# Decoder layer, last entry's self attention: where in the stage of scores the maxima's row transposes of two head groups stand

## Chip, core and metric

One core of a Trainium2 chip runs the whole kernel in one launch. The metric is the device time in microseconds (us), median of three executions. The engines are TensorE (PE; PEld is its weight load), VectorE (DVE), ScalarE (ACT), GpSimd (POOL) and SyncE (SP).

## What is computed

A decoder layer on `x` of 4 entries x 512 rows x 512 columns, float32: a causal self attention of 16 heads of 32 columns, a causal cross attention in which the context is both key and value (no projections), and a feed-forward part with a shared branch and one expert, each behind a layer norm and added to `x`. The part that the change touches is the self attention:

```python
q = (x @ q_w.T + q_b).reshape(Bd, Td, NH, HD).transpose(0, 2, 1, 3)
k = (x @ k_w.T + k_b).reshape(Bd, Td, NH, HD).transpose(0, 2, 1, 3)
v = (x @ v_w.T + v_b).reshape(Bd, Td, NH, HD).transpose(0, 2, 1, 3)
scores = jnp.einsum('bhqd,bhkd->bhqk', q, k) * SCALE
scores = jnp.where(causal, scores, -jnp.inf)
probs = jax.nn.softmax(scores, axis=-1)
ctx = jnp.einsum('bhqk,bhkd->bhqd', probs, v)
```

## The kernel before

The four entries (b = 0 to 3) run one after the other. The 16 heads of an entry form four groups g = 0 to 3 of four heads; 512 rows are four blocks of 128. The order of every engine's instructions is the order in which the program issues them: there is no scheduler, and an instruction that waits holds all that stands behind it on its engine.

An attention computes its scores twice, in two stages.

`with_maxima` is the stage of the maxima. For ten units of blocks it computes scores with query rows on the partitions (`sm`, L286), copies them to SBUF on ACT (L297), masks the diagonal on POOL (L305) and takes each row's maximum on DVE, negated (`nm`, L317). Between the units it places matmuls of other work as a filling. When the maxima of a group are complete, `split` (L339 to L343) on DVE writes each of them as three bfloat16 parts into `parts[g % 2]`. `rows(g)` then turns these parts into rows: four PE transposes of 128x128 into one PSUM tile (`mt`, L349) and one copy to SBUF (`mrow`, L355). Groups 0 and 1 are turned inside this stage, and group 2 too where the filling is long enough; `late` names the rest.

`attend` is the stage of the scores. It has ten units, here called u0 to u9, of blocks (g, j):

| unit | blocks | unit | blocks |
|---|---|---|---|
| u0 | (0,0) | u5 | (2,0) |
| u1 | (0,3) (0,1) | u6 | (2,3) (2,1) |
| u2 | (0,2) (1,2) | u7 | (2,2) (3,2) |
| u3 | (1,0) | u8 | (3,0) |
| u4 | (1,3) (1,1) | u9 | (3,3) (3,1) |

For each unit `scores` issues the transposed scores (`sc`, L383) in two PSUM tiles, a and b, adds `mrow` of the unit's groups by a matmul with ones (L394), takes the exponential on ACT (L414, into `pt`, or into `sum` for block 0 of groups 0 to 2), and masks the diagonal on POOL (L422). The values of unit n, here v0 to v9 (`pv`, L453), stand behind the scores of unit n + 2. The softmax denominators of groups 0 to 2 are summed first on DVE (`add_up`, L483: each block of a group is added into `sum`), and then over the partitions by one matmul with ones, `summed` (L489). `summed(0)` stands at the end of v2, `summed(1)` at the end of v5, `summed(2)` (`ls`) in v8.

`attend` issues the row transposes that `late` names right behind the scores of a unit, and their copy on ACT behind that unit's exponentials:

```python
for n, pieces in enumerate(units):
    waiting.append(a.scores(pieces))
    if n in late:
        for copy in a.rows(late[n]):
            copy(nc.scalar.copy)
    if len(waiting) > 2:
        values()
```

In entries 0 to 2 `late` is `{3: 3}`. In entry 3 the filling of the maxima stage is 16 matmuls for ten units, which is less than `2 * len(units)`, so group 2 is left for `attend` too.

All PSUM tiles come from one pool of four buffers of two banks each. A new tile takes the buffer that has been free longest, and its first writer on PE waits until the last reader of the old tile is done.

Of the kernel before, what the change touches and what calls it, by code (L numbers as in the profile page):

```python
# [26 lines left out]
def decoder_layer(  # L27
# [26 lines left out]
    NC = D // P  # L54
# [776 lines left out]
    def run(steps):  # L831
        for step in steps:
            for _ in step() or ():
                pass

    def matmuls(steps):

        for step in steps:
            yield from step() or ()
            yield  # L840

    def with_maxima(steps, a, first=0, norms=()):


        norms = list(norms)
        run(steps[:first])
        fill = matmuls(steps[first:])
        total = sum(1 if step.__name__ in ("share", "gate") else NC for step in steps[first:])

        units = []  # L850
        for g in range(0, NC, 2):
            units += [[(g, 1), (g + 1, 1)]]
            units += [u for k in (g, g + 1) for u in ([(k, 2), (k, 0)], [(k, NT - 1)])]

        lead = 2 if first else 0
        for _ in range(lead):
            next(fill)
        done, due, jobs, late = lead, float(lead), [], {3: NC - 1}
        for n, pieces in enumerate(units):
            new = a.maxima(pieces)  # L860
            if norms and n % 2 == 0:
                new.append(norms.pop(0))
            due += (total - lead) / len(units)

            count = round(due) - done
            for k in range(count):
                next(fill, None)
                done += 1
                if k == min(1, count - 1) and n in (5, 7):
                    jobs = a.rows((n - 5) // 2) + jobs  # L870
                if n == len(units) - 1 and k == count - (2 if count > 4 else 1):
                    if total >= 2 * len(units):
                        a.rows(2)[0](nc.scalar.copy)
                    else:
                        late[1] = 2
                run(jobs[:1])
                jobs = jobs[1:]
            run(jobs)
            jobs = new
        for _ in fill:  # L880
            pass
        run(jobs)
        return late
# [35 lines left out]
    with tc.manual_schedule(engines=BY_HAND):  # L919
# [11 lines left out]
        for b in range(B):  # L931
# [3 lines left out]
            if more:  # L935
                after, norms, turns = norm_in(b + 1)
            late = with_maxima(between_self, sa, skip, norms)
            if b == B - 1:
                e.x = load_x(b)
# [9 lines left out]
            ca = Attention(e.cq_t, e.ck_t, e.cv, True, f"c{b}")  # L949
            ca.e = e  # L950
            late = with_maxima(steps[3:], ca)
            if b + 2 < B:
                after.x = load_x(b + 1)
# [77 lines left out]
```

## Time and profile before

| | us |
|---|---|
| median of 3 runs | 814.12 (813.93 to 814.19) |
| the profiled execution, its own time | 814.14 |
| its span from first to last instruction | 812.4 |
| PE busy | 800.8 (99%) |
| DVE busy | 536.7 (66%) |
| ACT busy | 397.7 (49%) |
| POOL busy | 294.6 (36%) |
| from 620 to 636 us: PE, DVE, ACT, POOL busy | 13.37, 13.77, 13.22, 8.82 |
| from 636 to 653 us: PE, DVE, ACT, POOL busy | 17.00, 15.25, 10.65, 12.34 |

The stretch from 620.7 to 652.7 us is the stage of the scores of the last entry's self attention. The granted TensorE clock is 1.00 in all stretches. PE's busy share hides short waits, since the ends of matmuls are modelled and the groups overlap; a wait is found in the list of waits, in the gap that stands at the end of a row of the timeline, or by laying one entry's rows beside another's.

### The profile page before, as it was taken

What the parts mean: (1) busy time and instruction counts of PE and PEld (TensorE: products, weight loads), DVE (VectorE), ACT (ScalarE), POOL (GpSimd) and SP (SyncE); (2) the same over time, 40 slices, a digit from 0 to 9 for tenths busy, and PEclk for the clock granted to TensorE, in tenths of its full rate; (3) what the DMA queues carried; (4) which work ended last, traced back from release to release, by engine and by line L of the source; (5) the groups of instructions that cost most, each with busy time, mean ns of one, the idle gap of its engine ahead of it and who ended that gap; (6) DMA issues with size and microseconds to landing.
All of it is one profiled execution on the core that took longest, in us unless ns stands there. A gap on an engine that the chain in (4) does not pass through costs nothing.

```text
span 812.4 us, 14289 instructions
## 1 busy us (share of the span) xinstructions
PE 800.8 (99%) x5808; PEld 382.0 (47%) x5808; DVE 536.7 (66%) x927; ACT 397.7 (49%) x450; POOL 294.6 (36%) x489
## 2 busy tenths in 40 slices
PE   8999999999999999999999999999999999999998
PEld 7444554444444454444544445444444444444544
DVE  2478835868678834586867783687779844987512
ACT  2457426862546514556145752686168714574110
POOL 4334612342234732234233482244235643353100
PEclk9999999999999999999999999999999999999999
DMA  9611000001000000030100000000102000000101
GB/s 335 235 27 28 1 1 1 1 2 53 1 27 27 2 1 1 0 106 2 52 14 14 1 2 0 1 1 2 53 16 68 23 1 0 1 2 2 52 0 52
DMA packets 13681, 24.52 MB, mean 30 GB/s; under 512 B 1968, under 2 KB 2224, under 8 KB 13616
## 3 DMA queue, kind: packets, MB, share of 16 engines
q1 hardware_dynamic: 13184, 22.96, 8.3%
q8 instruction: 45, 0.74, 0.4%
q10 hardware_dynamic: 432, 0.66, 0.2%
q14 instruction: 20, 0.16, 0.1%
HBM read 19.42 MB, written 4.19 MB: 29 GB/s over the span
## 4 chain that ended last, share of the span: by engine, by line
PE 89%; DVE 8%; ACT 2%; DMA 0%; issue 0%; ACTq 0%
PE pm_qk L235 13%; PE pv_c L453 9%; PE pm_u L235 7%; PE pm_o L663 7%; PE pm_v L223 6%; PE pm_e L223 6%; PE sc_c L383 5%; PE pv_s L453 5%; PE pm_d L223 5%; PE sm_s L286 5%; PE sm_c L286 5%; PE sc_s L383 4%; DVE nm_s L317 3%; DVE nm_c L317 2%; PE sc_c L394 1%; PE sc_s L394 1%
## 5 line engine op out<-in xcount | busy, mean ns | idle before, releaser
L317 DVE TENSOR_REDUCE nm_c<-s_c 128x2 f32<-128x1024 f32 (+3 forms) x128 | 96.0, 811 | 37.4 <-POOL s_c L305 37.4
L317 DVE TENSOR_REDUCE nm_s<-s_s 128x2 f32<-128x1024 f32 (+3 forms) x128 | 96.9, 810 | 35.2 <-POOL s_s L305 35.2
L297 ACT COPY s_s<-sm_s 128x1024 f32<-128x1024 f32 x80 | 77.1, 1015 | 64.4 <-PE sm_s L286 34.9
L297 ACT COPY s_c<-sm_c 128x1024 f32<-128x1024 f32 x80 | 77.1, 1016 | 44.5 <-PE sm_c L286 24.5
L414 ACT ACTIVATE pt_c<-sc_c 128x1024 f32<-128x1024 f32 x80 | 76.7, 1030 | 30.1 <-PE sc_c L394 29.4
L305 POOL TENSOR_SCALAR_AFFINE_SELECT s_c<-s_c 128x512 f32<-128x512 f32 (+1 forms) x80 | 44.1, 552 | 115.0 <-ACT s_c L297 115.0
L422 POOL TENSOR_SCALAR_AFFINE_SELECT pt_c<-pt_c 128x512 f32<-128x512 f32 (+1 forms) x80 | 56.0, 706 | 67.0 <-ACT pt_c L414 66.5
L305 POOL TENSOR_SCALAR_AFFINE_SELECT s_s<-s_s 128x512 f32<-128x512 f32 (+1 forms) x80 | 43.8, 551 | 90.7 <-ACT s_s L297 90.7
L483 DVE TENSOR_TENSOR sum_s<-sum_s,pt_s 128x256 f32<-128x256 f32 (+2 forms) x72 | 58.7, 879 | 14.6 <-PE pv_s L453 14.6
L223 PE MATMUL pm_d<-wdown_sb,hT 128*128 128x512 f32 x128 | 60.9, 608 | 0.0
L414 ACT ACTIVATE pt_s<-sc_s 128x1024 f32<-128x1024 f32 x56 | 54.0, 1029 | 13.5 <-PE sc_s L394 7.9
L235 PE MATMUL pm_u<-fT,wup_sb 128*128 128x512 f32 x128 | 59.1, 605 | 0.0
L223 PE MATMUL pm_v<-wv_sb,xnT 128*128 128x512 f32 x128 | 58.8, 600 | 0.0
L663 PE MATMUL pm_o<-wo_sb,oT_s 128*128 128x512 f32 x128 | 57.8, 596 | 0.0
L235 PE MATMUL pm_qk<-xnT,wk_sb 128*128 128x512 f32 x120 | 57.3, 607 | 0.0
L223 PE MATMUL pm_e<-wexp_sb,fT 128*128 128x512 f32 x120 | 56.8, 606 | 0.0
L235 PE MATMUL pm_qk<-xnT,wq_sb 128*128 128x512 f32 x120 | 56.7, 604 | 0.0
L422 POOL TENSOR_SCALAR_AFFINE_SELECT pt_s<-pt_s 128x512 f32<-128x512 f32 (+1 forms) x56 | 47.5, 856 | 19.5 <-ACT pt_s L414 18.9
L383 PE MATMUL sc_s<-qT,kT 32*128 32x384 f32 (+3 forms) x512 | 53.0, 462 | 0.9 <-ACT sum_s L414 0.6
L383 PE MATMUL sc_c<-cqT,ckT 32*128 32x384 f32 (+3 forms) x512 | 51.4, 461 | 0.9 <-ACT pt_c L414 0.9
L286 PE MATMUL sm_s<-kT,qT 32*128 32x512 f32 (+3 forms) x512 | 47.5, 461 | 0.1
L286 PE MATMUL sm_c<-ckT,cqT 32*128 32x512 f32 (+3 forms) x512 | 46.1, 460 | 0.0
(154 smaller groups left out, 1199.8 us busy)
## 6 DMA issues: line engine op xcount, KB each, us to landing
cv<-in_ctx_dram SPq DMA_DIRECT2D x16, 256.0 KB, 4.2
out_dram<-x SPq DMA_DIRECT2D x15, 256.0 KB, 2.0
x<-in_x_dram SPq DMA_DIRECT2D x14, 256.0 KB, 3.6
xin<-in_x_dram SPq DMA_DIRECT2D x12, 256.0 KB, 2.7
wq_sb<-in_wq_dram SPq DMA_DIRECT2D x2, 512.0 KB, 6.3
wk_sb<-in_wk_dram SPq DMA_DIRECT2D x2, 512.0 KB, 7.9
wv_sb<-in_wv_dram SPq DMA_DIRECT2D x1, 1024.0 KB, 8.3
wo_sb<-in_wo_dram SPq DMA_DIRECT2D x1, 1024.0 KB, 10.0
```

What stands on the lines that cost most here:

```text
L223: nc.tensor.matmul(pm, lhsT=lhs_t[:, c, t * P : (t + 1) * P], rhs=w[:, c, :], start=(c == 0), stop=(c == NC - 1),)
L235: nc.tensor.matmul(pm, lhsT=w[:, c, f * P : (f + 1) * P], rhs=rhs_t[:, c, :], start=(c == 0), stop=(c == NC - 1),)
L286: nc.tensor.matmul(scs[r // 2][:, r % 2, c : c + (i + 1) * P], lhsT=self.q_t[h, g, i * P : (i + 1) * P], rhs=self.k_t[h, g, : (i + 1) * P] ...
L297: nc.scalar.copy(s, scs[n])
L305: nc.gpsimd.affine_select(out=diagonal, in_=diagonal, compare_op=ALU.is_ge, fill=NEG, base=0, pattern=[[0, 2], [0, len(pieces)], [-1, P]], ...
L317: nc.vector.tensor_reduce(self.nm[g][:, i, 2 * n : 2 * n + 2], made[n][:, :, c : c + (i + 1) * P], axis=AX.X, op=ALU.max, negate=True,)
L383: nc.tensor.matmul(scs[r // 2][:, r % 2, c : c + S - j * P], lhsT=self.k_t[h, g, j * P : (j + 1) * P], rhs=self.q_t[h, g, j * P :], start= ...
L414: nc.scalar.activation(pt, scs[n], AF.Exp)
L422: nc.gpsimd.affine_select(out=diagonal, in_=diagonal, compare_op=ALU.is_ge, fill=0.0, base=0, pattern=[[0, 2], [0, len(pieces)], [1, P]], ...
L453: nc.tensor.matmul(pv[r * HD : (r + 1) * HD, u, j * P :], lhsT=ones if u else self.v[:, j, h * HD : (h + 1) * HD], rhs=pts[r // 2][:, r % ...
L483: nc.vector.tensor_tensor(to, to, pts[n][:, :, c : c + S - j * P], ALU.add)
L663: nc.tensor.matmul(pms[t // 2][:, t % 2, :], lhsT=a.out[:, c, t * P : (t + 1) * P], rhs=wo_sb[:, c, :], start=(c == 0), stop=(c == NC - 1),)
```

## The change

In entry 3, and there alone, `late` goes from `{3: 3, 1: 2}` to `{3: 2, 5: 3}`. The four transposes of group 2 move on PE from behind the scores of u1 to behind those of u3, and the four of group 3 from behind u3 to behind u5; their two copies on ACT move with them. Group 2 is first used by u5 and group 3 by u7.

```diff
                 if n == len(units) - 1 and k == count - (2 if count > 4 else 1):
                     if total >= 2 * len(units):
                         a.rows(2)[0](nc.scalar.copy)
                     else:
-                        late[1] = 2
+                        late = {3: 2, 5: NC - 1}
```

No instruction is added or removed. The order on DVE, POOL and SP stays as it was; on PE two groups of four transposes move, on ACT two copies. The PSUM buffers of the tiles behind them are dealt out anew.

## Prediction

> **What bounds the kernel now.** I read the page first, then PE's waits, then the timelines of PE and DVE around the moved transposes, and last the same stage of entry 0, which has only one group of transposes in it.
>
> ```profile
> PE 800.8 (99%) x5808; PEld 382.0 (47%) x5808; DVE 536.7 (66%) x927; ACT 397.7 (49%) x450; POOL 294.6 (36%) x489
> PE 89%; DVE 8%; ACT 2%; DMA 0%; issue 0%; ACTq 0%
> ```
>
> PE is the bound nearly everywhere, so only time in which PE stands still, or work taken from PE, counts. The waits of PE:
>
> ```profile
> PE mt_s L349 <- DVE parts L343: 2.6, 2, 1.5
> ...
> PE sc_s L383 <- ACT sum_s L414: 0.6, 3, 0.2
> ```
>
> Both waits of the first line (2.6 us, two times) are the transposes that the change moves. PE's timeline there:
>
> ```profile
> 622.91 0.59 PE L394 MATMUL sc_s<-mrow_s,onesb 32*128 32x128 bf16 x8
> 624.60 0.40 PE L349 MATMUL mt_s<-identb,parts 128*128 128x128 bf16 x4 [1.10 <-DVE parts L343]
> ...
> 630.32 0.40 PE L349 MATMUL mt_s<-identb,parts 128*128 128x128 bf16 x4 [1.53 <-DVE parts L343]
> ...
> 631.65 1.15 PE L383 MATMUL sc_s<-qT,kT 32*128 32x128 f32 x16
> ...
> 632.95 1.07 PE L453 MATMUL pv_s<-pt_s,v 128*32 128x256 f32 x16
> 633.83 1.32 PE L489 MATMUL pv_s<-sum_s,ones 128*32 128x512 f32 x8
> 635.08 1.14 PE L383 MATMUL sc_s<-qT,kT 32*128 32x512 f32 x8
> ```
>
> PE stands 1.10 us before group 2 and 1.53 us before group 3. The line that decides, though, is L489, `summed(0)`: it takes 1.32 us here. What it reads comes from DVE:
>
> ```profile
> 624.42 4.71 DVE L317 TENSOR_REDUCE nm_s<-s_s 128x2 f32<-128x768 f32 x6
> 629.16 0.20 DVE L339 CAST parts<-nm_s 128x16 bf16<-128x16 f32 x1
> ...
> 630.14 3.91 DVE L483 TENSOR_TENSOR sum_s<-sum_s,pt_s 128x256 f32<-128x256 f32 x6
> 637.54 4.58 DVE L483 TENSOR_TENSOR sum_s<-sum_s,pt_s 128x512 f32<-128x512 f32 x6 [3.49 <-PE pv_s L453]
> ```
>
> DVE is behind: from 617.6 us on it works without a pause through the last maxima, then `split(3)`, then the six additions into `sum` of group 0, and ends at 630.14 + 3.91 = 634.05. L489 starts at 633.83, and its second half must wait for 634.05: that is its 1.32 us. So today both queues reach L489 together. PE's 2.63 us of waiting have cost it nothing that DVE would not have cost a little later. Entry 0, same stage:
>
> ```profile
> 73.86 0.40 PE L349 MATMUL mt_s<-identb,parts 128*128 128x128 bf16 x4
> ...
> 75.19 1.72 PE L383 MATMUL sc_s<-qT,kT 32*128 32x128 f32 x16
> ...
> 77.05 1.07 PE L453 MATMUL pv_s<-pt_s,v 128*32 128x256 f32 x16
> 77.94 1.04 PE L489 MATMUL pv_s<-sum_s,ones 128*32 128x512 f32 x8
> ```
>
> There DVE is in time, L489 takes 1.04 us, and from the first score (66.46) to L489 PE needs 11.48 us. But u4, behind the transposes, takes 1.86 us (75.19 to 77.05) where it takes 1.30 above (631.65 to 632.95): a transposes' tile occupies one of four PSUM buffers, so tile b of the next unit gets the buffer of tile b just before and waits for its exponential.
>
> **The change, part by part.** It removes and adds no instruction; DVE, POOL and SP keep their order and no DMA moves. All is set against the profiled execution (814.14 us, span 812.4; the median, 814.12, is the same within 0.02).
>
> 1. Both waits before the transposes go: -2.63 us of standing, for the moment. `split(2)` ends at 624.5 and `split(3)` at 630.3; the new places come at about 628 and 637.
>
> 2. PE up to L489. The order of PE from u0 to v2 is now that of entry 0, and the PSUM buffers repeat the same way. Entry 3's u0 starts at 620.72, its first exponential at 622.10; in entry 0 that is 67.84, so entry 0 shifted by 554.26 is the template: u2 at 623.2, transposes of group 2 at 628.1, u4 at 629.5, L489 at 77.94 + 554.26 = 632.20. PE arrives 1.63 us sooner than now; the rest of the 2.63 goes to the template's own waits for exponentials, 0.56 us of it in u4. The price of four transposes is 0.33 us on PE (630.32 to the next start), and one such group now lies before L489 instead of two.
>
> 3. DVE up to L489. The maxima do not move: a maximum of 128x1024 takes 1.21 us with a POOL mask beside it or without. `split` and the additions do care about POOL. Now u3's mask falls at 629.1 and 630.0 (entry 0: 74.87, 75.78), on `split(3)`: it took 1.10 us now, and the same four steps took 1.82 us in entry 0 beside two masks. Placed step by step against these masks I get 0.27 us more. The additions: six of them took 3.91 us here with one mask inside, 4.57 us in entry 0 with three, which is 0.2 to 0.3 us a mask. After the change u3's mask leaves them and u4's two come in (entry 0: 78.11, 79.02, so 632.4 and 633.3): one more, 0.22 us. The sum of group 0 is ready at 634.05 + 0.27 + 0.22 = 634.54.
>
> Here a rule speaks against the change. The Trainium skill, "SBUF — State Buffer", section "SBUF: two separate sides", says that VectorE with two SBUF inputs and GpSimd take a shared port pair by lock, for the whole instruction, and that the loser waits in full. The trace agrees for tiny operations: L341 took 1.20 us at 621.71, its usual 0.18 plus the rest of POOL's 1.27 us addition (L802). For the additions it does not: the rule would add up to a whole mask, 0.64 us, for each of two, 634.05 + 0.27 + 1.28 - 0.22 = 635.4; the rows say 634.5. I take the rows and keep the other for the range.
>
> 4. So PE waits at L489 for about 2 us instead, and u5 starts when the second half of L489 is through, as long after the sum as today: 635.08 + 0.49 = 635.57. The clock is no cost: it stayed at 1.00 after a stand of 2.00 us before the transposes at 8.34.
>
> 5. Transposes of group 3 behind u5: +0.33 us, now on the path, since they stand behind the new wait instead of before it.
>
> 6. Their PSUM tile. Behind the change u6 gets the two buffers of u5 (now it gets a free one and u5a's). From the transposes' start to v2 entry 0 took 77.05 - 73.86 = 3.19 us; today from u5's end (636.37) to v4 (638.83) it is 2.46. So transposes and stall cost 0.73 together, plus 0.18 because u5's exponentials start 0.10 us after that point (636.47) where u3's started 0.08 before: 0.91, of which 0.33 is counted. +0.58 us. The bounds are 0, if a buffer came free sooner, and the length of one exponential, 1.02.
>
> 7. L489 of group 1 (`summed(1)`, 642.09) took 1.06 us, of which some 0.09 was again DVE, ending at 637.54 + 4.58 = 642.12. PE now comes 1.4 us later, DVE 0.8: -0.09.
>
> 8. ACT's copies (0.59 us each): that of group 2 leaves the place before u2's exponentials, that of group 3 lies behind u5's and ends before u6's scores do. Nothing; 0.6 if it delayed u6's exponential. From u8 on PE has no gap in the timeline up to 713.57, so what is lost stays lost.
>
> Sum: 0.49 + 0.33 + 0.58 - 0.09 = +1.31 us, so 815.4.
>
> **Rivals.**
>
> A (forecast, 0.65): the wait moves to L489 and the late transposes cost what steps 5 and 6 say. Alone its range is 814.6 to 815.7 (DVE 0.2 to 0.7 later, stall 0.2 to 0.7).
>
> B (slower by more than 0.2%, 0.31): POOL's masks of u4 block DVE's additions at the rule's price. The sum of group 0 comes at 635.4, u5 at 636.4, and the total is 1.3 + 0.33 + 0.58 - 0.09 = +2.1 us, 816.2. It decides from a sum later than 634.9. For it: L341's 1.20 us, and an addition of 128x256 that took 1.5 us beside POOL's L504. Against it: the masks beside entry 0's additions.
>
> C (faster, 0.04): DVE catches up, L489 does not wait, and nothing takes the place of the 2.63 us: 811.5. With steps 2, 5 and 6 it would be -1.91 + 0.91 = -1.0, 813.1. Against it: DVE's row has no gap from 624.4 to 634.05 and its order is unchanged. That the change does nothing is excluded: PE's order differs.
>
> **Numbers.** A measurement of this kernel tells about 0.2%, 1.6 us, from no change; +1.31 lies within, close to the edge. Faster 0.04 (C), within 0.65 (A), slower 0.31 (B and A's upper end). The range 814.4 to 816.4 takes in A and B's price and leaves out C and a worse B.
>
> **What the profile would show.** Right: the waits of L349 on DVE in entry 3 are gone, a wait of about 2 us of L489 on `sum_s` L483 stands at 632 to 634.5, u5 starts near 635.6, u6's scores take about 1.9 us, the output projection starts near 654.0 instead of 652.68. Wrong: L489 of group 0 before 634; six additions of over 4.6 us (B); u6 in 1.4 us (step 6).

## Result and profile after

The changed kernel takes 815.71 us (median of 17 runs, 815.55 to 816.0) against 814.11 (17 runs, 813.93 to 814.31): +1.60 us, ratio 1.0020 with a 95% interval of 1.0012 to 1.0027. It is slower beyond its interval, and just inside the 0.2% that the prediction named as its edge. The forecast was 815.4 within 814.4 to 816.4.

The profiled execution took 816.0 us, the longest of the 17, and spans 814.3. Its first score of the stage stands at 620.98 where it stood at 620.72: 0.26 us were already lost at the very start (the first transposes came at 8.61 instead of 8.34), before anything that the change touches. Take 0.26 us off every place below to compare it with a place before.

The first line of the page, then two of PE's waits (waited for: total, times, longest):

```profile
PE 803.6 (99%) x5808; PEld 383.1 (47%) x5808; DVE 537.0 (66%) x927; ACT 397.7 (49%) x450; POOL 294.9 (36%) x489
```

```profile
PE pv_s L489 <- DVE sum_s L483: 1.4, 1, 1.4
PE sc_s L383 <- ACT sum_s L414: 1.1, 5, 0.3
```

The line of L349 on `parts` is gone. In its place stands one of L489 on the sum, and the waits of scores for exponentials grew from 0.6 us in three places to 1.1 in five. PE's timeline:

```profile
628.41 0.40 PE L349 MATMUL mt_s<-identb,parts 128*128 128x128 bf16 x4
...
634.12 2.09 PE L489 MATMUL pv_s<-sum_s,ones 128*32 128x512 f32 x8 [1.44 <-DVE sum_s L483]
636.14 1.14 PE L383 MATMUL sc_s<-qT,kT 32*128 32x512 f32 x8
...
637.43 0.40 PE L349 MATMUL mt_s<-identb,parts 128*128 128x128 bf16 x4
...
638.75 0.49 PE L383 MATMUL sc_s<-qT,kT 32*128 32x128 f32 x4
639.51 1.14 PE L383 MATMUL sc_s<-qT,kT 32*128 32x128 f32 x12 [0.27 <-ACT sum_s L414]
...
640.79 1.07 PE L453 MATMUL pv_s<-pt_s,v 128*32 128x128 f32 x16
```

PE arrives at L489 early, stands for 1.44 us, does the first half, and stands again before the second (2.09 us instead of 1.32). u5 starts at 636.14, the transposes of group 3 take their 0.33 us behind it, and u6 breaks after four matmuls until an exponential frees a PSUM buffer. DVE in the same stretch:

```profile
629.42 0.20 DVE L339 CAST parts<-nm_s 128x16 bf16<-128x16 f32 x1
...
630.21 0.23 DVE L343 TENSOR_TENSOR parts<-rest_s,parts 128x16 bf16<-128x16 f32 x1
630.31 4.79 DVE L483 TENSOR_TENSOR sum_s<-sum_s,pt_s 128x256 f32<-128x256 f32 x6
```

POOL beside the additions, before and after:

```profile
630.68 0.49 POOL L422 TENSOR_SCALAR_AFFINE_SELECT sum_s<-sum_s 128x256 f32<-128x256 f32 x1 [0.49 <-ACT sum_s L414]
```

```profile
630.34 0.68 POOL L422 TENSOR_SCALAR_AFFINE_SELECT sum_s<-sum_s 128x256 f32<-128x256 f32 x1 [0.43 <-ACT sum_s L414]
632.66 1.90 POOL L422 TENSOR_SCALAR_AFFINE_SELECT pt_s<-pt_s 128x512 f32<-128x512 f32 x2 [1.65 <-ACT pt_s L414]
```

The six additions took 4.79 us instead of 3.91. The second mask of u3 lies beside them as it did before. New are the two masks of u4, alone 0.64 us each: they lie over the end of the additions, and it is 1.90 us from the start of the first to the end of the second. The chain of work that ended last (start, us, what) says the same:

```profile
632.95 1.13 DVE sum_s L483
634.07 0.04 issue
634.12 2.09 PE pv_s L489 x8
...
637.54 1.93 ACT sum_s L414 x2
```

After the maxima and `split(3)` it now runs over DVE's additions into L489, and then through ACT's exponentials of u5 into u6. Neither was on the chain before, which went from `split(3)` to PE at 630.32 and stayed on PE through this stage.

### The profile page after: what moved, and what is told of

It reads as the page before. It is cut to its first block, busy times and chain, and to the rows that moved or that the text cites. A ratio compares the mean times of both kernels' runs of the same rounds, so it can differ in the third digit from the quotient of the medians.

```text
span 814.3 us, 14289 instructions
## 1 busy us (share of the span) xinstructions
PE 803.6 (99%) x5808; PEld 383.1 (47%) x5808; DVE 537.0 (66%) x927; ACT 397.7 (49%) x450; POOL 294.9 (36%) x489
## 4 chain that ended last, share of the span: by engine, by line
PE 89%; DVE 8%; ACT 2%; issue 0%; DMA 0%; ACTq 0%
PE pm_qk L235 13%; PE pv_c L453 9%; PE pm_u L235 7%; PE pm_o L663 7%; PE pm_v L223 6%; PE pm_e L223 6%; PE sc_c L383 5%; PE pm_d L223 5%; PE pv_s L453 5%; PE sm_s L286 5%; PE sm_c L286 5%; PE sc_s L383 4%; DVE nm_s L317 3%; DVE nm_c L317 2%; ACT sum_s L414 1%; PE sc_c L394 1%
## 5 line engine op out<-in xcount | busy, mean ns | idle before, releaser
L383 PE MATMUL sc_s<-qT,kT 32*128 32x128 f32 (+3 forms) x512 | 54.7, 463 | 1.5 <-ACT sum_s L414 1.1
```

What stands on the lines that cost most here:

```text
L383: nc.tensor.matmul(scs[r // 2][:, r % 2, c : c + S - j * P], lhsT=self.k_t[h, g, j * P : (j + 1) * P], rhs=self.q_t[h, g, j * P :], start= ...
```

## Experiments

All times are medians; the kernel before was run beside each and gave 814.13 or 814.14 us. "Theory A" is the prediction's: the sum of group 0 on DVE sets the start of u5, and what stands on PE before L489 is free. The first score of the stage starts at 620.56 to 620.98 us in these profiles, with nothing changed ahead of it, so a place is given from there where a few tenths matter.

### Group 3's transposes one unit sooner

```diff
-                        late = {3: 2, 5: NC - 1}
+                        late = {3: 2, 4: NC - 1}
```

> Late is {3: 2, 4: 3}: group 3's transposes stand behind u4, before the wait of L489, instead of behind u5. Theory A (DVE's sum of group 0 sets the start of u5; the transposes cost only where they stand behind that wait): their 0.33 us and the PSUM stall of u6 of 0.55 us disappear in the wait, so 815.7 - 0.9 = 814.8; L489 still waits for L483, by 0.33 us less, and u5 starts where it starts after the change. Rival (DVE is no bound, PE pays for every transpose and buffer wherever it stands): 815.7.

814.89 us, ratio 1.0010 (1.0002 to 1.0018): 0.82 less than the change. PE's timeline:

```profile
631.36 0.40 PE L349 MATMUL mt_s<-identb,parts 128*128 128x128 bf16 x4
631.69 1.35 PE L453 MATMUL pv_s<-pt_s,v 128*32 128x256 f32 x16
633.86 2.09 PE L489 MATMUL pv_s<-sum_s,ones 128*32 128x512 f32 x8 [0.83 <-DVE sum_s L483]
...
638.17 1.31 PE L383 MATMUL sc_s<-qT,kT 32*128 32x128 f32 x16
```

The transposes and a stall of some 0.3 us behind them (v2 takes 1.35 us instead of 1.07) go into the wait of L489, which shrinks from 1.44 to 0.83; u6 runs in one piece. Steps 5 and 6 of the prediction, the transposes and their PSUM tile, are thereby shown together: the late place costs 0.82 us, and the same work before the wait costs nothing. The 0.76 us over the kernel before that remain are left to DVE, whose additions take 4.79 us here too.

### Group 2 behind u2, group 3 left behind u3

```diff
-                        late = {3: 2, 5: NC - 1}
+                        late = {2: 2, 3: NC - 1}
```

> Late is {2: 2, 3: 3}: group 2's transposes go from behind u1 to behind u2, group 3's stay behind u3 as before the change. Theory A: the wait of 1.10 us goes, but PE then stands longer before group 3, until split(3) ends near 630.3, and L489 comes when it came: 814.1 within 0.3. Rival (each wait is PE time and is won when it goes): 814.1 - 1.1 = 813.0.

814.26 us, ratio 1.0001 (0.9993 to 1.0009). PE's waits, then its timeline:

```profile
PE mt_s L349 <- DVE parts L343: 0.7, 1, 0.7
```

```profile
633.50 1.54 PE L489 MATMUL pv_s<-sum_s,ones 128*32 128x512 f32 x8
634.97 1.14 PE L383 MATMUL sc_s<-qT,kT 32*128 32x512 f32 x8
```

1.9 us of the 2.6 us of waiting for `parts` are gone, and the time has not moved: u5 starts 14.41 us after the stage's first score, where it started 14.36 after it. These waits were worth nothing while DVE's sum stood behind them.

### Group 3 moved alone

```diff
-                        late = {3: 2, 5: NC - 1}
+                        late = {1: 2, 5: NC - 1}
```

> Late is {1: 2, 5: 3}: group 2's transposes where they stood before the change, group 3's where the change puts them. Theory A (DVE's sum of group 0 sets u5, and the loss comes from group 3's late place and from u4's masks, which come early enough to fall on the additions): PE still stands about 1.1 us before group 2, L489 waits for L483, u6's scores stall by 0.55 us, and the time is that of the whole change, 815.6. Rival (each moved group gives half of the loss): 814.9.

815.94 us, ratio 1.0028 (1.0018 to 1.0039). Three of its eight runs took 817.4, the other five 815.69 to 816.01; the profiled one took 815.70. PE's waits:

```profile
PE pv_s L489 <- DVE sum_s L483: 1.8, 1, 1.8
...
PE mt_s L349 <- DVE parts L343: 1.1, 1, 1.1
```

With group 2 back in its old place, and its old wait of 1.1 us back, the loss is whole. It is not half and half: moving group 3 alone gives all of it. That puts group 3's transposes behind the end of the sum, and it takes from PE the wait before u4, so that u4's masks come sooner and fall on the additions (4.79 us here too).

### No additions into the sum of group 0

```diff
-                if g in self.added:
+                if g in self.added and (g, self.name) != (0, "s3"):
                     for n in range(2):
```

> The changed kernel without the additions into the sum of group 0 in the last entry (left out: six DVE additions, so that entry's group 0 is divided by too small a sum). Theory A: L489 has nothing to wait for, PE runs as in entry 0, u5 starts 1.9 us before where it started before the change, and the late transposes and the stall of u6 add 0.9: 814.1 - 1.9 + 0.9 - 0.1 = 813.0. Rival (the cost sits on PE and in PSUM buffers alone, DVE is hidden): 815.7.

813.18 us, ratio 0.9988 (0.9981 to 0.9994).

```profile
632.23 1.04 PE L489 MATMUL pv_s<-sum_s,ones 128*32 128x512 f32 x8
633.20 1.22 PE L383 MATMUL sc_s<-qT,kT 32*128 32x512 f32 x8
```

This kernel leaves the six additions out. L489 starts at 632.23; entry 0 as a template (its stage shifted by 554.26 us) had said 632.20. So PE's order in the changed kernel is as short as the template says, and 2.53 us of the changed kernel's time hang on the six additions. The time stays only 0.95 us below the kernel before: u5 starts 1.88 us sooner than there, and the late transposes with the break of u6 take 0.91 back.

### No masks of u4

```diff
             for n in range(2):
                 ...
                 nc.scalar.activation(pt, scs[n], AF.Exp)
                 ...
+                if self.name == "s3" and (g, j) == (1, 3):
+                    pts.append(pt)
+                    continue
```

> The changed kernel without POOL's two masks of u4 in the last entry (left out: the diagonal mask of blocks (1,3) and (1,1)). It prices POOL beside DVE's additions. At the prediction's rows (0.22 us for one mask more): 815.5. At the two rows of the trace after, where the last two additions took 1.12 us each instead of 0.68: 0.88 us, 814.8. At a full block of each mask: 1.28 us, 814.4.

814.91 us, ratio 1.0009 (1.0000 to 1.0017): 0.80 less than the change.

```profile
630.23 3.91 DVE L486 TENSOR_TENSOR sum_s<-sum_s,pt_s 128x256 f32<-128x256 f32 x6
```

```profile
630.26 0.67 POOL L425 TENSOR_SCALAR_AFFINE_SELECT sum_s<-sum_s 128x256 f32<-128x256 f32 x1 [0.44 <-ACT sum_s L414]
```

This kernel leaves POOL's two masks of u4 out. The additions (L486 here) are back at 3.91 us, with a mask of u3 still beside them (L425). So u4's two masks cost them 0.88 us, twice the 0.44 that the prediction charged for the two, and 0.80 of it reaches the end.

### split(3) behind the sum

```diff
+        held = jobs.pop() if 2 in late.values() else None
         run(jobs)
-        return late
+        return late, held
             ...
             if len(waiting) > 2:
                 values()
+            if n == 3 and held_split:
+                held_split()
```

`held` is `split(3)`, and `held_split` is the same in `attend`.

> The changed kernel with split(3) on DVE moved behind the six additions into the sum of group 0; its result is first needed by the transposes behind u5. Theory A: the sum is ready 1.0 us sooner (split(3) took 1.02 us), u5 follows, 815.7 - 1.0 = 814.7, and the transposes of group 3 do not wait. Rival (the additions then meet u3's masks too, or the transposes wait for split(3) again, and DVE's order gives nothing): 815.5.

813.73 us, ratio 0.9995 (0.9987 to 1.0004): 1.98 less than the change, where 1.0 was expected. DVE's timeline, then POOL's:

```profile
629.31 3.69 DVE L483 TENSOR_TENSOR sum_s<-sum_s,pt_s 128x256 f32<-128x256 f32 x6
```

```profile
629.42 3.89 POOL L422 TENSOR_SCALAR_AFFINE_SELECT sum_s<-sum_s 128x256 f32<-128x256 f32 x1 [0.45 <-ACT sum_s L414]
```

The sum is ready at 629.31 + 3.69 = 633.00, 2.10 sooner than in the changed kernel (630.31 + 4.79 = 635.10). 1.0 of it is `split(3)`; 1.1 is that POOL did not get in between: u3's first mask, 0.42 us alone, began 0.11 us after the first addition and ended only 0.3 us after the last, and POOL's later masks came behind it. PE's list has no wait for DVE in this stage any more; L489, with 1.60 us from 632.50, still holds a short one between its halves.

### POOL's two additions of entry 1 put off

In the kernel before, `split(2)` meets two POOL additions of entry 1 (L802). They and the output behind them are kept in a list and issued behind u9's masks, and the load of `x` goes behind them (the diff leaves out the output's and the list's own lines):

```diff
-            nc.gpsimd.tensor_tensor(xt, xt, some, ALU.add)
+            if b == B - 3:
+                later.append(lambda: nc.gpsimd.tensor_tensor(xt, xt, some, ALU.add))
+            else:
+                nc.gpsimd.tensor_tensor(xt, xt, some, ALU.add)
             ...
-            if b == B - 1:
-                e.x = load_x(b)
             attend(sa, late)
+            if b == B - 1:
+                e.x = load_x(b)
```

> The kernel before, with entry 1's two POOL additions (L802, 2.49 us together, just before the scores of entry 3) and the output DMAs behind them put off to the end of that stage, behind the masks of u9; entry 3's load of x goes behind them. Theory A: L341 and L342 of split(2) took 1.20 us each beside these additions and take 0.2 alone, so DVE is 2.0 us sooner from there on: no wait before group 2, hardly one before group 3, sum of group 0 near 632.5, u5 about 1.3 us sooner, 812.8. Rival (POOL's additions only stand beside DVE's backlog): 814.1. A cost at the other end (the load of x comes late for the bias addition): over 814.1.

812.98 us, ratio 0.9986 (0.9980 to 0.9993). DVE's timeline, then PE's:

```profile
621.61 0.18 DVE L341 TENSOR_TENSOR rest_s<-nm_s,parts 128x16 f32<-128x16 f32 x1
621.83 0.20 DVE L342 CAST parts<-rest_s 128x16 bf16<-128x16 f32 x1
...
628.17 4.57 DVE L483 TENSOR_TENSOR sum_s<-sum_s,pt_s 128x256 f32<-128x256 f32 x6
```

```profile
632.73 1.13 PE L489 MATMUL pv_s<-sum_s,ones 128*32 128x512 f32 x8
```

Two operations that took 1.20 and 1.21 us take 0.18 and 0.20, DVE is 1.9 us sooner at the sum's start (counted from the stage's first score), and neither group's transposes wait, in the places of before. Two instructions on a lightly loaded engine had held the stage back by 1.2 us. The transfers moved too, and no run moved them alone: the DMA share from 620 to 636 us fell from 0.29 to 0.01. For the additions as the cause speaks that in the kernel before the two DVE operations ended at 622.91 and 624.15, right behind POOL's additions, which ended at 622.87 and 624.09.

### The same with three other places for the transposes

```diff
-                        late[1] = 2
+                        late = {3: 2, 4: NC - 1}
```

This is the first of the three. The second has the change's own `{3: 2, 5: NC - 1}`; in the third `attend` takes two groups for one unit, `{4: (2, NC - 1)}`.

> The same put-off of entry 1's POOL additions, with late {3: 2, 4: 3} in place of {3: 3, 1: 2}. Theory A: L489 then waits for DVE little or not at all, both groups of transposes stand before it as in the kernel with the put-off alone, and neither finds its parts missing: 812.6, within 0.3 of that kernel. Rival (transposes behind u4 keep a PSUM buffer from u5 when nothing else holds u5): 813.2.

812.92 us, ratio 0.9985 (0.9978 to 0.9991), the fastest of all, but not to be told from the run before it.

> The put-off of entry 1's POOL additions, with the late places of the change, {3: 2, 5: 3}. Theory A: DVE is in time, so L489 does not wait, but group 3's transposes stand behind u5 and u6's scores stall on their PSUM tile: against {3: 2, 4: 3} with the put-off (812.92) 0.33 us leave the place behind u4, and 0.33 + 0.55 come behind u5: 813.5, faster than the kernel before by 0.6 but slower than the put-off with the places of before (812.98). Rival (the places do not matter once DVE is in time): 812.9.

813.65 us, ratio 0.9993 (0.9985 to 1.0001). With DVE nearly in time the change's own places still cost 0.7 us against the best. u5 starts 13.05 us after the first score, as it does in the best (13.06), so the loss comes behind it. PE's timeline shows both late costs again:

```profile
634.93 0.40 PE L349 MATMUL mt_s<-identb,parts 128*128 128x128 bf16 x4
...
637.02 1.14 PE L383 MATMUL sc_s<-qT,kT 32*128 32x128 f32 x12 [0.27 <-ACT sum_s L414]
```

> The put-off of entry 1's POOL additions, with both groups of transposes behind u4. Theory A: each of their tiles takes one of four PSUM buffers; behind u3 that costs u4 some 0.56 us of waiting for an exponential, behind u4 the next tiles are those of the values and of u5, which come later: 812.92 - 0.5 = 812.4. Rival (two tiles at once leave u5 too few buffers and the stall goes there): 812.9 to 813.2.

813.41 us, ratio 0.9990 (0.9982 to 0.9998): a miss, and slower than the rival had it.

```profile
630.62 0.40 PE L349 MATMUL mt_s<-identb,parts 128*128 128x128 bf16 x4
631.78 0.38 PE L349 MATMUL mt_s<-identb,parts 128*128 128x128 bf16 x4 [0.77 <-DVE sum_s L483]
```

u4 does run without its stall, but the second tile of transposes needs a PSUM buffer at once and waits. The view names an addition on DVE as the releaser; `split(3)` had ended at 628.9, and what ended just before 631.78 is the exponential of u4a (ACT, 630.71 to some 631.73), so I read it as the buffer. The stall was moved, not removed. More than half of the loss is DVE's again, though:

```profile
633.16 1.33 PE L489 MATMUL pv_s<-sum_s,ones 128*32 128x512 f32 x8
```

```profile
628.81 4.58 DVE L483 TENSOR_TENSOR sum_s<-sum_s,pt_s 128x256 f32<-128x256 f32 x6
```

u4's masks come sooner, one of them falls on the additions (4.58 us; 4.13 with group 3 behind u4), and L489 waits in its second half. Counted from the first score, L489 starts 0.15 us later than in the best run, and takes 1.33 us where it took 1.04 there; the two make 0.44 of the 0.49 us.

## Why the prediction was right, and where it was off

Each term as the prediction had it, and as the two profiled executions give it with the 0.26 us taken off:

| term | predicted | measured | from |
|---|---|---|---|
| DVE's sum later, and with it u5 | +0.49 | +0.80 | 635.08 to 636.14 |
| of it `split(3)` | +0.27 | -0.08 | 1.10 to 1.02 |
| of it the six additions | +0.22 | +0.88 | 3.91 to 4.79 |
| transposes of group 3 behind u5 | +0.33 | +0.32 | 637.43 to 637.75 |
| stall of u6 on PSUM | +0.58 | +0.58 | v4 at 638.83 to 640.79, less the two above |
| second stall of DVE gone | -0.09 | -0.08 | u8 at 643.15 to 645.03 |
| sum | +1.31 | +1.62 | runs: +1.60 |

**The mechanism was right.** The two waits went, a wait at L489 took their place, and nothing of the 2.6 us reached the end. The run without the additions confirms entry 0 as the template (L489 at 632.23), and the one with group 2 behind u2 confirms that the waits in PE's list were worth nothing.

**The term that was mis-sized is step 3, the additions: +0.22 forecast, +0.88 measured.** I charged u4's two masks at 0.22 us each and took off 0.22 for a mask of u3 that was to leave the additions. Neither held. u4's masks are of 128x512, and each costs 0.44: the last two of the six additions took 1.12 us instead of 0.68, and the run without these masks has the 0.88 back. And u3's second mask did not leave. It came within 0.04 us of the place that I had worked out, but `split(3)` was held for only 0.09 us in one step, so the additions began 0.03 us before that mask. The kernel before held both prices, in entry 0:

```profile
73.19 4.57 DVE L483 TENSOR_TENSOR sum_s<-sum_s,pt_s 128x256 f32<-128x256 f32 x6
```

```profile
73.52 0.92 POOL L422 TENSOR_SCALAR_AFFINE_SELECT pt_s<-pt_s 128x512 f32<-128x512 f32 x1 [0.28 <-ACT pt_s L414]
74.87 0.66 POOL L422 TENSOR_SCALAR_AFFINE_SELECT sum_s<-sum_s 128x256 f32<-128x256 f32 x1 [0.43 <-ACT sum_s L414]
75.78 0.83 POOL L422 TENSOR_SCALAR_AFFINE_SELECT sum_s<-sum_s 128x256 f32<-128x256 f32 x1 [0.25 <-ACT sum_s L414]
```

Its three masks are not alike: one is of 128x512. The additions with one mask (3.91) and with these three (4.57) differ by one mask of each size, 0.66 us, so the mean is 0.33 a mask and not "0.2 to 0.3". L341, which I took as agreeing with the rule, is short of it too: 0.18 us plus the 1.15 us that POOL's addition still had to run make 1.33, and it took 1.20.

**Luck had a part in it.** The additions were 0.66 us too small and `split(3)` 0.35 us too large, so DVE's term missed by only 0.31; its 0.80 us lies outside the 0.2 to 0.7 that A allowed, and 815.71 is the upper end of A's own range. That A's side of the 0.2% came true, by 0.03 us (1.60 measured, edge 1.63, and an interval that goes past it), is luck. One sign of being wrong was met to the letter: L489 starts at 633.86 in the prediction's time, before 634. It does so because its first half needs only a part of the sum, and the wait that the sign was to rule out is there, in front of it and in it.

**Rival B was half right.** It said that the rule which it quotes would block the additions in full and put the sum at 635.4 and the time at 816.2. In the prediction's time the sum came at 634.84, between the rows' 634.54 and the rule's 635.4; B was to decide from 634.9. One of its marks, six additions of over 4.6 us, came true. For a mask of u4, which takes 0.64 us alone, neither 0.22 nor the full 0.64 is the price here, but 0.44.

**Rival C** would have needed DVE to be in time. Without the additions the time was 813.18; C with steps 2, 5 and 6 said 813.1.

## What to carry to other kernels

A wait on the busiest engine is worth only the distance to the next thing that engine waits for. Before taking it away, look a few rows further for a consumer of the same late engine, here L489, and compare that row's duration with the same line where the engine is in time. Work that must stand somewhere is free before such a wait and paid for behind it, its PSUM tile included. And when a lagging engine sets the time, look for what another engine holds from it: putting two POOL additions off gave 1.2 us, where none of the four other places tried for PE's transposes gained anything without it.

## What the runs showed of the hardware

A maximum on DVE (128x1024, one input) took 1.21 us beside a POOL mask and without one. A cast or a subtraction of 128x16 took 1.20 us beside POOL's additions and 0.2 without. An addition of 128x512 took 1.12 us beside a mask of the same size and 0.68 without.

The six additions took 3.69 us where no mask got in. In the last entry of every other run that has them, and in entry 0, they took, to within 0.01 us, 0.22 us more for each mask of 128x256, and 0.44 more for each of 128x512, that came in before the last addition began: 3.91 with one small mask (the kernel before), 4.13 with two (group 3 behind u4, POOL's additions put off), 4.57 with two small and one large (entry 0), 4.79 with one small and two large (the change). Alone these masks take 0.42 and 0.64 us, 0.20 more than they cost; no run shows why.

In the run with `split(3)` behind the sum, six additions that follow each other without a gap kept one 0.42 us mask out for 3.89 us and were not slowed at all. In the changed kernel, where a mask began 0.03 us after the first addition, it was over after 0.68 us, inside the second addition, which took 0.64 us instead of 0.41. Which of the two engines gets in is not settled: what decides it was not tried.

The granted clock was 1.00 from 620 to 636 us of the changed kernel, with PE's stand before L489 in it.
